# Folding the sums of four scans into the last scan's own accumulation, with the turning, the norm's bias and the sign bytes rearranged

## The chip, the cores and the metric

One core of one Trainium2 chip. The metric is the device time of one execution in microseconds (us). Every time below is a median of several executions; all of them were in the fast state. A verdict of "faster" or "slower" needs 2%.

## The reference, cut to what matters

A vision block on 4 images of 64 x 64 pixels and 96 channels: a sign-quantized projection to 192 channels, a 3 x 3 convolution, a selective scan over the 4096 pixels in four directions, a norm, a gate and another quantized projection; then an attention block and a feed-forward block, which the change does not touch.

```python
x_flat = xconv.reshape(Bn, Dn, L)
x_tr = xconv.transpose(0, 1, 3, 2).reshape(Bn, Dn, L)          # columns first
xs = concatenate([x_hwwh, flip(x_hwwh)], axis=1)               # four directions
h = dA * h + (dt * ut)[..., None] * Bt[:, :, None, :]          # the scan, 16 states
y = einsum('bkdn,bkn->bkd', h, Ct)                             # sum over the states
out_y = y + D[None, :, :, None] * u
...
y = out_y[:, 0] + inv_y[:, 0] + wh_y + invwh_y                 # the four directions
y = (y - mu) / sqrt(var + 1e-05) * ln_w + ln_b
y = y * silu(z)
return bilinear(y, W_out, s_out, b_out)                        # signs of y only
```

## The kernel before

One loop runs over 1536 pieces: 4 images, 4 directions in the order 1, 3, 0, 2, 4 chunks of 1024 pixels, 6 groups of 32 channels, 4 quarters of the states. A piece is: ScalarE (ACT) makes the decay `dA`, GpSimd (POOL) the input product, VectorE (DVE) the scan, DVE or POOL the product with C, and TensorE (PE) sums the states in PSUM (`yp`). After every eighth piece ACT copies `yp` out (`ys`) and DMAs store it to `yd`. All loads of the loop are issued on one queue, SyncE's (SP).

```python
def reduce(self, i):                       # state sums of one piece
    ...
    for x in range(4):
        c.nc.tensor.matmul(y[32 * x : 32 * x + 32, g % 2, :], c.sum4, prod[:, 256 * x : 256 * x + 256],
            start=(q == 0), stop=(q == NQ - 1), tile_position=(0, 32 * x))

def run(self, back):
    ...
    for i in range(n):
        self.at = i
        self.loads(i)                      # every 4th piece: two loads of 512 KB (dl), a few groups ahead
        if i >= 1: self.carry(i - 1)
        if i + 1 < n: self.decay(i + 1)    # ACT
        ...                                # evacuate, reduce, inject
        self.scan(i)                       # DVE
        ...
        interleave(lanes)
        next(back, None)                   # one step of the background work
```

`back` is the background: convolution and signs of the image after next (`prologue`), turning two directions back into row order (`turn`), and the eight sums of each image (`norm`, 512 pixels each), one step per piece. When the scans are over, what is left runs alone.

```python
# prologue: the signs, two bytes of a pair apart
nc.scalar.activation(sg.bitcast(F8).rearrange("p (h e i) -> p h i e", h=8, e=2),
                     pz.rearrange("p (h i e) -> p h i e", h=8, e=2), AF.Sign, saturate=False)

# turn: y1 + y3 by two products with the identity, then a strided copy out of PSUM
for i, t in enumerate(ts):
    nc.tensor.matmul(ps, c.i96, t, start=(i == 0), stop=(i == 1))
yield
nc.scalar.copy(yh.rearrange("p (h w) -> p h w", w=IW)[:, :, 8 * q : 8 * q + 8],
               ps.rearrange("p (w h) -> p h w", h=IH))

# norm, inside the scans: four products and a copy for each half
mm(ps, [(c.i96, x["y0"][:, h]), (c.i96, x["y2"][:, h]), (c.i96, x["y13"][:, h]), (c.dskip[:, h], x["u"][:, h])])
yield
nc.scalar.copy(t, ps)                      # ysum
...
mm(ps, [(c.meanw[:, 0, h], ys[0]), (c.meanw[:, 1, h], ys[1]), (c.lnb[:, h], sd)])   # sy
```

Of the kernel before, what the change touches and what calls it, by code (L numbers as in the profile page):

```python
# [37 lines left out]

KORD = (1, 3, 0, 2)
AHEAD = 4  # L40

# [9 lines left out]
def hybrid_kernel(ctx: ExitStack, tc: tile.TileContext, a: dict, out: bass.AP):  # L51
# [4 lines left out]
    def pool(name, bufs, **kw):  # L56
# [4 lines left out]
        w=pool("wp", 9), y=pool("yp", 2), cy=pool("cyp", 2), h=pool("hp", 2), pu=pool("pup", 1), pd=pool("pdp", 2),  # L61
# [80 lines left out]
    mean, meanw = ctile("mean", [96, 2, 96]), ctile("meanw", [96, 2, 2, 96])  # L142
    dskip, lnb = ctile("dskip", [96, 2, 96]), ctile("lnb", [96, 2, 96])
    on192, on96, mean96 = ctile("on192", [96, 96]), ctile("on96", [96, 96]), ctile("mean96", [96, 96])
# [6 lines left out]

    tts = [ctile(f"tt{i}", [DM + 1, 512]) for i in range(2)]

    def weights():
# [62 lines left out]
        for rows, h, s in halves(a["pv"][:, :, LN_W]):  # L217
            nc.sync.dma_start(wrow[:, h, rows], s.partition_broadcast(96))
        small = {}
# [26 lines left out]
        for tt in tts:  # L246
            nc.gpsimd.memset(tt[DM : DM + 1, :], 1.0)
# [94 lines left out]
        for h in range(2):  # L342
            for o in range(2):
                nc.vector.tensor_tensor(meanw[:, h, o], mean[:, int(h != o)], wrow[:, o], ALU.mult)
            nc.vector.tensor_scalar(dskip[:, h], i96, dsum[:, h : h + 1], None, ALU.mult)
            nc.vector.tensor_scalar(lnb[:, h], i96, pv[:, h, LN_B : LN_B + 1], None, ALU.mult)
# [11 lines left out]
    c.ready, c.later = set(), Later(nc)  # L358
# [56 lines left out]
def run(c):  # L415

    made, first = c.weights(), prologue(c, 0, c.xts)
    lanes = [made, first]
    while (0, 1) not in c.ready:
        interleave(lanes)  # L420
        c.later.tick()
    scans = Scans(c)
    ends = [Epilogue(c, b, scans) for b in range(NB)]

    def back():

        yield from first
        yield from prologue(c, 1)
        for b in range(NB):
            if b + 2 < NB:  # L430
                yield from prologue(c, b + 2)
            while not scans.done(b, 2):
                yield
            yield from turn(c, b)
            e = ends[b]
            e.open()
            yield from e.sums(e.lane)
            if b + 1 < NB:
                yield from e.middle()
                yield from e.last(e.lane)  # L440
                e.close()

    behind = back()
    scans.run(behind)


    def drain(lanes):
        while lanes:
            interleave(lanes)
            c.later.tick()  # L450
        c.later.flush()

    e = ends[-1]
    e.alone = True
    more = [e.spare_lane(x) for x in range(2)]
    drain([behind] + [e.sums(ln) for ln in more])
    drain([e.middle()])
    drain([e.last(ln) for ln in [e.lane] + more])
    e.close()


def prologue(c, b, xts=None):
# [11 lines left out]
    with tc.tile_pool(name=f"xg_{b}", bufs=1) as xgp:  # L474
# [4 lines left out]
        with tc.tile_pool(name=f"cv_{b}", bufs=1) as cvp:  # L479
# [72 lines left out]
            for n, part in enumerate(parts + [None]):  # L552
# [5 lines left out]
                for s in range(3):  # L558
# [8 lines left out]
                    if prev:  # L567
# [4 lines left out]
                        elif s == 1:  # L572
# [3 lines left out]
                                sg.bitcast(F8).rearrange("p (h e i) -> p h i e", h=8, e=2),  # L576
                                pz.rearrange("p (h i e) -> p h i e", h=8, e=2), AF.Sign, saturate=False,
# [145 lines left out]
def turn(c, b):  # L723

    nc, tc, p = c.nc, c.tc, c.p

    def load(h, q):
        ts = []
        for k in (1, 3):
            t = p.f.tile([128, 512], F32, name=f"yt{h}{q}{k}_{b}", tag="f")[0:96]  # L730
            nc.sync.dma_start(t, c.yd[k][b][96 * h : 96 * h + 96, 512 * q : 512 * q + 512])
            ts.append(t)
        return ts

    with tc.tile_pool(name=f"tn_{b}", bufs=1) as tn:
        for h in range(2):
            yh = tn.tile([96, L], F32, name=f"yh{h}_{b}", tag="yh")
            nxt = load(h, 0)
            for q in range(NQ8):
                ts, nxt = nxt, load(h, q + 1) if q + 1 < NQ8 else None  # L740
                yield
                ps = p.ps.tile([128, 512], F32, name=f"tn{h}{q}_{b}", tag=f"b{q % 2}")[0:96]
                for i, t in enumerate(ts):
                    nc.tensor.matmul(ps, c.i96, t, start=(i == 0), stop=(i == 1))  # L744
                yield
                nc.scalar.copy(
                    yh.rearrange("p (h w) -> p h w", w=IW)[:, :, 8 * q : 8 * q + 8],
                    ps.rearrange("p (w h) -> p h w", h=IH),
                )
            nc.sync.dma_start(c.y13[b][h], yh)  # L750
            yield


class Epilogue:
# [9 lines left out]
    def open(self):  # L764
        c, p, b = self.c, self.c.p, self.b
        ep = self.ep = self.ctx.enter_context(c.tc.tile_pool(name=f"ep_{b}", bufs=1))
        self.vks = ep.tile([DM, DM], F32, name=f"vks_{b}", tag="vks")
        self.ms = [ep.tile([DM + (i == 2), DM], F32, name=f"m{i}_{b}", tag=f"m{i}") for i in range(3)]
        self.lane = SimpleNamespace(
            f32=lambda nm: p.f.tile([128, 512], F32, name=f"{nm}_{b}", tag="f"),  # L770
            bank=lambda nm, j: p.ps.tile([128, 512], F32, name=f"{nm}_{b}", tag=f"b{j}"),
            load=lambda key, nm, shape, dt=F32: ep.tile(shape, dt, name=f"{nm}_{b}", tag=key),
            tts=c.tts, x={},
        )
        self.opened = True
# [4 lines left out]
    def spare_lane(self, n):  # L780
# [14 lines left out]
        for i, nm in enumerate(("y0", "y2", "y13", "u")):  # L795
            views[nm] = big[i][0:96].rearrange("p (h l) -> p h l", h=2)
# [12 lines left out]
    def take(self):  # L809
# [4 lines left out]
        if self.scans.at <= (self.b * NK + NK - 1) * NPC + NG * NQ * (ci + 1) + 16:  # L814
            return None
        return self.todo.pop(0)

    def loads(self, ln, q, names):
        c, b = self.c, self.b
        cols = slice(512 * q, 512 * q + 512)  # L820
        for nm in names:
            src, shape, dt = {
                "y0": (c.yd[0][b].rearrange("(h p) l -> p h l", h=2), [96, 2, 512], F32),
                "y2": (c.yd[2][b].rearrange("(h p) l -> p h l", h=2), [96, 2, 512], F32),
                "y13": (c.y13[b].rearrange("h p l -> p h l"), [96, 2, 512], F32),
                "u": (c.ud[b].rearrange("h p l -> p h l"), [96, 2, 512], F32),
# [4 lines left out]
            c.nc.sync.dma_start(t, src[..., cols])  # L831
# [13 lines left out]
    def sums(self, ln):  # L845
        nxt = None
        while nxt is not None or self.todo or not self.opened:
            q, nxt = nxt, None
            if q is None:
# [4 lines left out]
                self.loads(ln, q, ("y0", "y2", "y13", "u", "sz", "xb"))  # L854
# [6 lines left out]
    def norm(self, ln, q, got):  # L861
# [9 lines left out]
        ys = []  # L871
        if self.alone:
            nc.gpsimd.tensor_tensor(x["y0"], x["y0"], x["y2"], ALU.add)
            for h in range(2):
                c.vec.scalar_tensor_tensor(
                    x["y13"][:, h], x["u"][:, h], c.dsum[:, h : h + 1], x["y13"][:, h], ALU.mult, ALU.add
                )
            for h in range(2):
                t = f32(f"ysum{h}")
                c.vec.tensor_tensor(t, x["y0"][:, h], x["y13"][:, h], ALU.add)  # L880
                ys.append(t)
            yield
        else:
            for h in range(2):
                ps = bank(f"ys{h}", h)[0:96]
                mm(ps, [(c.i96, x["y0"][:, h]), (c.i96, x["y2"][:, h]), (c.i96, x["y13"][:, h]), (c.dskip[:, h], x["u"][:, h])])
                yield
                t = f32(f"ysum{h}")
                nc.scalar.copy(t, ps)
                ys.append(t)  # L890
        nxt = self.take()
        got.append(nxt)
        if nxt is not None:
            sz, xb = x["sz"], x["xb"]
            self.loads(ln, nxt, ("y0", "y2", "y13", "u"))
        sz, xb = x["sz"], x["xb"]
        sq = []
        if self.alone:
            ps = bank("mu", 0)[0:96]
            mm(ps, [(c.on192, ys[0]), (c.on192, ys[1])])  # L900
# [16 lines left out]
        ps = bank("var", int(self.alone))[0:96]  # L917
# [5 lines left out]
        sd = f32("sd")  # L923
        nc.scalar.activation(sd, ps, AF.Ln, bias=c.eps5[0:96])
# [3 lines left out]
        if self.alone:  # L928
# [4 lines left out]
            gs = yc  # L933
        else:
            for h in range(2):
                ps = bank(f"sy{h}", 1 - h)[0:96]
                mm(ps, [(c.meanw[:, 0, h], ys[0]), (c.meanw[:, 1, h], ys[1]), (c.lnb[:, h], sd)])
                sy.append(ps)
            yield
            yield  # L940
# [5 lines left out]
        yield  # L946
        gt = []
# [144 lines left out]
class Scans:  # L1092
# [6 lines left out]
    def __init__(self, c):  # L1099
# [9 lines left out]
        self.us, self.gs, self.at, self.loaded = {}, {}, -1, set()  # L1109

    def done(self, b, n):

        return self.at > (b * NK + n) * NPC + 16
# [141 lines left out]

    def reduce(self, i):
# [5 lines left out]
        y, prod = self.ydone[i // 8], self.ins.pop(i)  # L1262
        for x in range(4):
            c.nc.tensor.matmul(  # L1264
                y[32 * x : 32 * x + 32, g % 2, :], c.sum4, prod[:, 256 * x : 256 * x + 256],
                start=(q == 0), stop=(q == NQ - 1), tile_position=(0, 32 * x),
            )

# [14 lines left out]
    def run(self, back):  # L1283
# [25 lines left out]
        for i in range(n):  # L1309
            self.at = i  # L1310
            self.loads(i)
            if i >= 1:
                self.carry(i - 1)
            if i + 1 < n:
                self.decay(i + 1)
            full = i % 8 == 3 and i > 8
            if full:
                self.evacuate(i - 4)
            elif i >= 3:
# [11 lines left out]
            if full:  # L1331
                self.reduce(i - 3)
# [81 lines left out]
```

## Time and profile before

| | before |
|---|---|
| median of 3 runs | 5783.25 us (5775.27 to 5783.98) |
| profiled execution: span | 5775.5 us, mean granted clock 0.672 |
| up to the first scan of the loop | 287.9 us |
| the 1536 pieces | 5321.9 us |
| after the last scan (the tail) | 165.7 us |

The two engines that fill the loop are DVE and POOL; the prediction below shows the lines. What is worth keeping in mind when reading them: in the loop both engines are busy some 5025 us, so the time between 5025 and 5322 us is the most that a change can win there if it leaves the work of these two as it is.

A direction is 96 pieces. From the starts of the scan instructions in the time line I took the time of each of the 16 directions, and put together the first three directions of each image and its last one, which is where the change adds work:

| us, profile of before | image 0 | image 1 | image 2 | image 3 | sum |
|---|---|---|---|---|---|
| first three directions | 1021.3 | 1018.9 | 996.4 | 961.7 | 3998.3 |
| last direction | 339.5 | 335.2 | 329.8 | 319.1 | 1323.6 |

### The profile page before, as it was taken

How to read it: one execution, taken by the hardware profiler on the slowest of the kernel's cores; microseconds unless marked ns; L12 is line 12 of the kernel's file. 1: busy time of each engine (PE TensorE's matmuls, PEld its weight loads, DVE VectorE, ACT ScalarE, POOL GpSimd, SP SyncE). 2: the span in 40 equal slices, each digit the busy share in tenths (PEclk: the TensorE clock that was granted, in tenths of full speed). 3: DMA queues.
4: the chain of work that ended last, by engine and by line, in shares of the span. 5: the costliest groups of instructions: out<-in, count | busy, mean ns of one | idle time of the engine just before them, and what ended most of it. 6: DMA issues, size and time to landing. Idle time of an engine off the chain costs nothing. (4 is left out here: it accounts for less than half of the span.)

```text
span 5775.5 us, 61921 instructions
## 1 busy us (share of the span) xinstructions
PE 3419.4 (59%) x19813; PEld 1339.9 (23%) x19813; DVE 5176.7 (90%) x3422; ACT 3672.1 (64%) x5620; POOL 5080.7 (88%) x2291
## 2 busy tenths in 40 slices
PE   6446645664468755666446875563477654353577
PEld 3222222222223322222212322221122211111123
DVE  3299999999889999999999999999999999999984
ACT  5567876886556566788655656755556676554544
POOL 2099999999889999999998999999999999999980
PEclk8666755676678866666567885565688765565687
DMA  4455656655676655665567665575667555575652
GB/s 75 105 169 189 196 180 200 194 170 178 200 222 213 205 177 176 204 189 164 184 218 226 209 206 177 182 223 190 207 195 214 191 189 185 174 222 180 197 160 73
DMA packets 589452, 1069.91 MB, mean 185 GB/s; under 512 B 225867, under 2 KB 295556, under 8 KB 587332
## 3 DMA queue, kind: packets, MB, share of 16 engines
q1 hardware_dynamic: 575636, 1065.88, 59.3%
q8 instruction: 156, 2.56, 0.2%
q10 hardware_dynamic: 13488, 0.07, 0.1%
q14 instruction: 172, 1.41, 0.1%
HBM read 833.20 MB, written 229.38 MB: 184 GB/s over the span
## 5 line engine op out<-in xcount | busy, mean ns | idle before, releaser
L386 POOL TENSOR_TENSOR w<-dl,bc 128x1024 f32<-128x1024 f32 x1536 | 3578.4, 2354 | 149.2 <-PE yp L1264 73.8
L1223 ACT ACTIVATE dA<-dl,anm 128x1024 f32<-128x1024 f32 x1536 | 1714.0, 1116 | 494.6 <-DVE w L386 254.6
L1264 PE MATMUL yp<-w,sum 128*32 128x256 f32 x12288 | 1323.3, 547 | 845.8 <-ACT ys L1276 447.7
L386 DVE TENSOR_TENSOR_SCAN dA<-dA,cy,w 128x1024 f32<-128x1024 f32 x680 | 1593.1, 2343 | 109.7 <-ACT dA L1223 94.0
L386 POOL TENSOR_TENSOR w<-h,bc 128x1024 f32<-128x1024 f32 x631 | 1483.8, 2352 | 191.6 <-DVE h L386 181.0
L386 DVE TENSOR_TENSOR w<-dA,bc 128x1024 f32<-128x1024 f32 x905 | 1108.6, 1225 | 57.9 <-DVE dA L386 0.9
L386 DVE TENSOR_TENSOR_SCAN h<-dA,cy,w 128x1024 f32<-128x1024 f32 x472 | 1103.8, 2340 | 12.0 <-ACT dA L1223 10.2
L1264 PEld LDWEIGHTS yp<-w,sum 128*32 128x32 f32 x12288 | 363.1, 137 | 1941.0 <-issue 836.8
L386 DVE TENSOR_TENSOR_SCAN dA<-dA,w 128x1024 f32<-128x1024 f32 x225 | 513.6, 2283 | 38.3 <-ACT dA L1223 29.9
L1254 ACT COPY cy<-dA 128x1 f32<-128x1 f32 x680 | 105.8, 156 | 666.2 <-DVE w L386 665.7
L562 PE MATMUL cv<-tp,cw 96*96 96x512 fp8e5 x1152 | 390.8, 499 | 137.5 <-ACT r L611 110.0
L386 DVE TENSOR_TENSOR_SCAN h<-dA,w 128x1024 f32<-128x1024 f32 x159 | 362.3, 2279 | 32.0 <-POOL w L386 23.7
L562 PEld LDWEIGHTS <-cw 96*96 96x96 fp8e5 x1152 | 174.3, 158 | 358.2 <-issue 314.6
L744 PE MATMUL tn<-yt,ident 96*96 96x512 f32 x256 | 175.1, 820 | 111.8 <-DMA yt<-yd 111.1
L836 PE MATMUL ys<-ey,ident 96*96 96x512 f32 x336 | 184.7, 692 | 75.2 <-DMA ey<-yd 47.4
L1254 ACT COPY cy<-h 128x1 f32<-128x1 f32 x472 | 87.6, 186 | 193.5 <-DVE h L386 193.5
L575 ACT ACTIVATE sg<-cz 96x512 fp8e5<-96x512 f32 x64 | 159.0, 2484 | 22.1 <-DVE cz L386 22.0
L1166 ACT ACTIVATE pd<-dps,dbias,pvd 128x512 f32<-128x512 f32 x189 | 143.7, 760 | 23.1 <-PE dps L1161 23.1
L386 DVE TENSOR_TENSOR u<-cz,e 96x512 f32<-96x512 f32 x64 | 43.8, 684 | 115.6 <-ACT e L586 108.6
L1167 ACT ACTIVATE sp<-dps,dbias,pvd 128x512 f32<-128x512 f32 x189 | 144.6, 765 | 0.0
L836 PE MATMUL fc<-x,mean 96*96 96x512 f32 x54 | 51.9, 1064 | 151.9 <-DVE x L386 151.9
L386 DVE TENSOR_TENSOR pd<-dps,pu 128x512 f32<-128x512 f32 x189 | 130.7, 691 | 8.6 <-DMA pu<-ud 2.2
(305 smaller groups left out, 4448.1 us busy)
## 6 DMA issues: line engine op xcount, KB each, us to landing
dl<-dld SPq DMA_DIRECT2D x768, 512.0 KB
bc<-bcd SPq DMA_DIRECT2D x512, 512.0 KB
dld<-pd SPq DMA_DIRECT2D x126, 512.0 KB
yd<-ys SPq DMA_DIRECT2D x768, 64.0 KB
dld<-pd SPq DMA_DIRECT2D x126, 256.0 KB
yt<-yd SPq DMA_DIRECT2D x128, 192.0 KB
ey<-yd SPq DMA_DIRECT2D x58, 384.0 KB
pu<-ud SPq DMA_DIRECT2D x32, 512.0 KB
```

Source lines behind the costliest of these rows:

```text
L386: return getattr(self.eng, name)(out, *args, **kw)
L562: nc.tensor.matmul(ps, c.cw[:, j, t, 96 * h : 96 * h + 96], tpad[j][:, 8 * q + dy : 8 * q + dy + 8, dx : dx + IW], start=(j == 0 and t == ...
L575: nc.scalar.activation(sg.bitcast(F8).rearrange("p (h e i) -> p h i e", h=8, e=2), pz.rearrange("p (h i e) -> p h i e", h=8, e=2), AF.Sign ...
L744: nc.tensor.matmul(ps, c.i96, t, start=(i == 0), stop=(i == 1))
L836: self.c.nc.tensor.matmul(ps, w, x, start=(i == 0), stop=(i == len(pairs) - 1))
L1166: nc.scalar.activation(d[:, 0], ps, AF.Abs, scale=sc, bias=bi)
L1167: nc.scalar.activation(t, ps, AF.Relu, scale=sc, bias=bi)
L1223: c.nc.scalar.activation(t, self.dlt[i // NQ][0], AF.Exp, scale=c.anm[:, g, NQ * KORD[e] + q : NQ * KORD[e] + q + 1])
L1254: self.c.nc.scalar.copy(self.carries[g, q], h[:, CH - 1 : CH])
L1264: c.nc.tensor.matmul(y[32 * x : 32 * x + 32, g % 2, :], c.sum4, prod[:, 256 * x : 256 * x + 256], start=(q == 0), stop=(q == NQ - 1), tile ...
```

## The change

Its intent is to take work off ACT and PE inside the loop. The last direction's state sums are already being accumulated in PSUM; the y of the other directions and D u are added there by a few more products, so that the sum of all four directions is stored as `yd[2]` and the norm needs one load and no sum of its own. Five parts:

1. Sign bytes in order: `sg` is written contiguously, PSUM is read with a step of two.
2. `load_sums`: in direction 3 the y of direction 1 is added (one product per group), in direction 2 y0, the turned y and u D (three products). `ysum` goes.
3. Turning without products: `yh` is copied straight from the loaded tile, which holds y1 + y3 already.
4. The norm's bias is row 97 of the product `sy` and not a product of its own.
5. Order and tail: sums may start 8 pieces after their chunk instead of 16, and in the last 64 pieces the background takes two steps per piece. Two more turns of order belong here: `turn` now comes ahead of `prologue` of the image after next, not behind it, and the copy `ys` stands ahead of the next decay in ACT's order, not behind it. No run takes either of these two alone.

```diff
-    sg.bitcast(F8).rearrange("p (h e i) -> p h i e", h=8, e=2),
-    pz.rearrange("p (h i e) -> p h i e", h=8, e=2), AF.Sign, saturate=False,
+    sg.bitcast(F8).rearrange("p (h e i) -> p h e i", h=8, e=2),
+    pz.rearrange("p (h i e) -> p h e i", h=8, e=2), AF.Sign, saturate=False,
 ...
+    def load_sums(self, i):
+        b, e, ci, g, q = self.pieces[i]
+        k = KORD[e]
+        if k < 2:
+            return
+        at = CH * (NCH - 1 - ci)
+        t = c.p.ya.tile([128, 3, 256], F32, name=f"ya_{i}", tag="ya")          # pool of one buffer
+        srcs = [c.yd[1][b]] if k == 3 else [c.yd[0][b], whole(c.y13[b]), whole(c.ud[b])]
+        for j, src in enumerate(srcs):
+            c.nc.sync.dma_start(t[:, j], src[32 * g : 32 * g + 32, at : at + CH].rearrange("d (x l) -> x d l", x=4))
+        self.sums[i // NQ] = [(t[:, j, ::-1], c.dskip[:, g] if j == 2 else c.back4) for j in range(len(srcs))]
 ...  # reduce
+        for n, (src, w) in enumerate(more):
+            c.nc.tensor.matmul(y[:, g % 2, :], w, src, start=False, stop=(n == len(more) - 1))
 ...  # run
             self.loads(i)
+            if i % NQ == NQ - 1:
+                ...
+                self.load_sums(i)
 ...
+            if i % 8 == 3 and i > 8:
+                self.evacuate(i - 4)           # the copy ys, now ahead of self.decay(i + 1)
 ...
             next(back, None)
-            if full:
-                self.reduce(i - 3)
+            if i > n - 64:
+                next(back, None)
 ...  # turn
-                for i, t in enumerate(ts):
-                    nc.tensor.matmul(ps, c.i96, t, start=(i == 0), stop=(i == 1))
-                yield
-                nc.scalar.copy(yh..., ps.rearrange("p (w h) -> p h w", h=IH))
+            nc.scalar.copy(yh..., ts.pop(0).rearrange("p (w h) -> p h w", h=IH))
+            if n + 3 < len(parts):
+                ts.append(load(*parts[n + 3]))
 ...  # norm
-                mm(ps, [(c.i96, x["y0"][:, h]), (c.i96, x["y2"][:, h]), (c.i96, x["y13"][:, h]), (c.dskip[:, h], x["u"][:, h])])
-                nc.scalar.copy(t, ps)
-                mm(ps, [(c.meanw[:, 0, h], ys[0]), (c.meanw[:, 1, h], ys[1]), (c.lnb[:, h], sd)])
+                mm(ps, [(c.meanw[0:96, 1, h], ys[1]), (c.meanw[:, 0, h], y0)])
```

## The prediction

> **What bounds the kernel now.** I read the page's busy line first, then the windows of three stretches (start, scans, tail), then the 16 windows of one scan direction each, then who waited for whom, then the time line around single stalls and of the tail.
>
> ```profile
> PE 3419.4 (59%) x19813; PEld 1339.9 (23%) x19813; DVE 5176.7 (90%) x3422; ACT 3672.1 (64%) x5620; POOL 5080.7 (88%) x2291
> ```
>
> ```profile
> 0.00:285.00 285.00, 152.84 (x711) 87.71 (x712) 74.94 (x135) 148.86 (x197) 41.14 (x104) 0.75 0.40 87
> 285.00:5613.00 5328.00, 3160.13 (x18778) 1204.93 (x18777) 5027.10 (x3152) 3457.35 (x5312) 5029.11 (x2181) 0.67 0.61 193
> 5613.00:5776.00 163.00, 106.46 (x332) 47.31 (x324) 74.70 (x135) 65.87 (x112) 10.49 (x7) 0.72 0.33 89
> ```
>
> The columns are length, then busy time and instructions of PE, PEld, DVE, ACT, POOL. The 1536 scan pieces take 5328 us (3.47 us each). DVE is busy 5027 of them and POOL 5029: both are full and balanced, and each lies idle 5.6%. The start (285 us) and the tail (163 us) stand alone. So the time is 5030 us of DVE and POOL work that this change hardly touches, about 300 us of their gaps, and 448 us of ends. Of the 16 directions the worst is the last of image 0, with the turning and the first state sums behind it, and the best has nearly nothing behind it:
>
> ```profile
> 1286.00:1618.00 332.00, 155.59 (x1204) 65.58 (x1206) 299.30 (x181) 208.77 (x324) 299.75 (x131) 0.61 0.62 190
> 4613.00:4945.00 332.00, 161.76 (x1054) 57.64 (x1054) 323.08 (x199) 215.57 (x339) 322.95 (x140) 0.61 0.55 182
> ```
>
> DVE idles 33 us in the first and 9 in the second. If all 16 were like the best, 16 x 9 = 144 of the 300 us would stay, so background work can cost about 150 us at most. The waits inside the scans say through whom:
>
> ```profile
> DVE dA L386 <- ACT dA L1223: 123.9, 82, 8.5
> DVE u L386 <- ACT e L586: 44.3, 28, 3.4
> ...
> ACT ysum L889 <- PE ys L836: 138.9, 52, 11.0
> ACT yh L746 <- PE tn L744: 44.6, 18, 10.6
> ```
>
> ACT is 64% busy yet late: it takes its work in order, so a copy that waits for PE holds back the next decay (dA), and DVE has two dA buffers only. One such stall in full, at the first sum of image 0:
>
> ```profile
> 1675.12 5.40 PE L836 MATMUL ys<-ey,ident 96*96 96x512 f32 x6 [10.46 <-DMA ey<-yd]
> ...
> 1681.55 0.58 ACT L889 COPY ysum<-ys 96x512 f32<-96x512 f32 x1 [9.60 <-DMA dld<-pd]
> ...
> 1683.31 2.30 DVE L386 TENSOR_TENSOR_SCAN dA<-dA,w 128x1024 f32<-128x1024 f32 x1 [7.04 <-ACT dA L1223]
> ```
>
> PE waits for the six loads, ACT for PE, DVE for ACT. I went through all DVE waits on ACT in the scans (209 us) in the time line and sorted them by the ACT idle just ahead: a copy of ysum 67 us (48 waits), u behind the sign bytes 44 us (28), a copy of yh 18 us, plain ones with no such cause 44 us, others the rest.
>
> **What the Trainium skill says.** "Perfetto Trace Analysis", section Identifying the Most-Contended Engine: for Vector and GPSIMD occupancy is a fair measure of the distance to the roof; here both stand at 94% within the scans, which agrees with a small possible gain. "SBUF — State Buffer", section Door 1: The DMA port swizzle: SBUF is accessed in 16-byte lines and an access that moves to a new line each time is penalised. The trace agrees:
>
> ```profile
> L575 ACT ACTIVATE sg<-cz 96x512 fp8e5<-96x512 f32 x64 | 159.0, 2484 | 22.1 <-DVE cz L386 22.0
> L598 ACT COPY ut<-u 96x512 f32<-96x512 f32 x48 | 52.9, 1101 | 41.9 <-DVE u L386 41.9
> L746 ACT COPY yh<-tn 96x512 f32<-96x512 f32 x64 | 36.9, 577 | 54.4 <-PE tn L744 44.6 <-DMA bc<-bcd 6.8 <-issue 3.0
> ```
>
> sg writes single bytes 32 bytes apart (2484 ns, against 770 for other fp8 results); ut reads SBUF 256 bytes apart (1101); yh reads PSUM in the same stride without a penalty (577). "FP8 and Floating Point Precision", section TensorE Precision Notes: true fp32 takes 4 passes. The trace agrees: an fp32 product of 512 columns shows as two records, 0.43 us each at the faster clock.
>
> **The change part by part.**
> 1. Sign bytes in order: 64 x sg. The bytes are now written in order and PSUM is read with a step of two. Busy time should fall from 2484 to 770-950 ns; in the time line its slot falls from 1.95 us (131.56 to 133.52) to about 0.65, so 1.3 us each. In the scans the 28 waits of u shrink by up to 1.3 us: 44 to about 11, **-33**. In the start the loop of the 16 convolution parts is 7.45 us, of which the ACT and DVE chain (0.77 r, 0.94, 1.95 sg, 0.95, 0.66, 0.66, u 0.69, v 0.81) makes all; shortened it is 6.15. But PE's own loop is the convolution plus about 1.9, and the convolution takes 4.08 us in some parts, 5.8 to 7.4 in the others. Only the fast parts gain: **-6**.
> 2. State sums into the scans' PSUM: the 4 fp32 products and the copy of ysum, per half and 512 columns, go (56 copies x 581 ns of ACT, 246 us of PE records), with their 67 us of DVE stalls. What takes their place is the wait of the square for yc and the first load: I keep 17 us, **-50**. Added: 96 groups in direction 3 with one product and 96 in direction 2 with three, 384 fp32 products of 128 x 256, an estimate of 0.43 to 0.85 us each by the passes, 165 to 330 us of PE, against 478 that go with turning (175), ys (246) and the bias (57). Loads: 384 x 128 KB = 50 MB come, 12.6 (turning) and 29 x 3 x 384 KB = 34 MB go; a wash. The new load is asked for three pieces (10.4 us) ahead and has one buffer; PE will wait for it at times, and POOL and ACT have about three pieces of slack: **+10**.
> 3. Turning without products: 64 yh copies read SBUF in a 256-byte stride, so like ut 1.10 instead of 0.58 us: +34 us of ACT, and ACT itself waits for the load. The lead from load to copy is three pieces as before, so its 18 us of DVE stalls stay: **0**.
> 4. Bias as a row: 57 us of PE off the path, the sy product has 97 rows: **0**.
> 5. Order and tail. Before, four of image 3's eight sums are left at the last scan (yc of four is seen before 5590), so the tail has a round of three and a round of one:
>
> ```profile
> 5613.43 0.58 ACT L1276 COPY ys<-yp 128x512 f32<-128x512 f32 x1 [4.35 <-PE yp L1264]
> ...
> 5675.31 0.25 DVE L386 TENSOR_TENSOR vks<-vk,vks 96x96 f32<-96x96 f32 x1
> ...
> 5698.78 0.25 DVE L386 TENSOR_TENSOR vks<-ln0ps,vks 96x96 f32<-96x96 f32 x1 [5.64 <-PE ln0ps L836]
> ```
>
> A sum has 13 yields before and 11 after, the settling time is 8 pieces instead of 16, and the last 64 pieces take two steps each. By counting, sums 7 to 2 finish inside the scans and two are left: one round. Loads from 5616 land by about 5620, and a lone round takes 27 us (5672 to 5699) less 3 for the adds, plus 6 for two lanes: done near 5650 instead of 5699: **-45**. The last stage (76 us) is unchanged. The price is norm work at twice the pace: about 17 us of PE in 5.5 pieces beside the scans' products, and ACT waiting within one piece: **+15** for six sums.
>
> The scans' DVE gains, 33 + 50 = 83, count for 70, because POOL lies idle for other reasons too (74 us for PE). Sum: -70 + 10 + 15 - 45 - 6 = -96. 5783 - 96 = 5687; I say **5690 us**.
>
> **Rivals.** (a) The stalls move instead of going: ACT now waits for loads in turning, the square waits for yc and ys. For it: every stall above 7 us began at a load. Then -40 in place of -70, and with the tail 5720. (b) The double pace at the end costs what the tail gains: each step that waits within its own piece can cost DVE 1 to 2 us, five such steps in six sums are 40. Then about 5715. (c) The added sums are late in PE: the product frees late, POOL starves and ACT's copy of the state sums, now ahead of the decay, stalls. For it: 23 waits of PE for the turning loads, up to 13.7 us. Against it: three pieces of slack. 192 groups at 0.5 us would be +96: no gain. (d) Relief of PE and ACT reaches nearly all of the 150 us that the background costs: -120 in the scans, 5640.
>
> **Range and chances.** Most of the sum is certain in sign; sizes are not. With (d) and a cheap tail 5620; with (a) and (b) together 5745. 2% is 116 us, below 5668, 22 us past my middle: faster 0.31, same 0.67, slower 0.02.
>
> **What would show it.** sg near 0.8-0.95 us; yh near 1.1; no ysum and no tn; scans' DVE idle near 220 us and u's wait on e near 11; new waits of PE yp on ya few and below 10 us; two sums after the last scan and the tail near 118 us instead of 163; the start near 279. It is wrong if DVE's wait for dA stays at 124 (rival a), if the idle in the last 64 pieces passes 30 us (b), or if POOL waits for PE above 74 (c).

## The result, and the profile after

The changed kernel takes 5724.14 us (median of 4 runs, 5703.31 to 5737.8) against 5782.82 us (4 runs) before. The ratio is 0.9898, with a 95% interval of 0.9865 to 0.9931: about 1% faster, within the 2%. A ratio is the mean time of one kernel's fast runs over that of the other's fast runs of the same rounds, so it is not quite the ratio of the medians. The changed kernel's runs scatter over 34 us, before's over 9; the profiled execution (5737.8 us) is the slowest of the four, so stretches read from it are up to some 15 us long in all. The start varies little, 259 to 269 us in all profiles with the signs in order, and the tail with the double pace 118 to 124, so most of these 15 us are probably in the loop.

First the busy line of the page of the changed kernel, then the windows of its start, its loop, its tail and the last 64 pieces (columns as in the prediction: length, busy time and instructions of PE, PEld, DVE, ACT and POOL, granted clock, DMA share, GB/s):

```profile
PE 3345.6 (58%) x19813; PEld 1357.2 (24%) x19813; DVE 5154.9 (90%) x3396; ACT 3566.8 (62%) x5564; POOL 5075.9 (88%) x2295
```

```profile
0.00:267.10 267.10, 144.55 (x739) 85.76 (x740) 78.04 (x139) 121.38 (x198) 42.32 (x104) 0.78 0.44 96
267.10:5613.80 5346.70, 3112.89 (x18796) 1231.45 (x18795) 5025.60 (x3161) 3393.00 (x5278) 5029.30 (x2188) 0.65 0.61 194
5613.80:5736.00 122.20, 88.19 (x278) 39.98 (x278) 51.23 (x96) 52.44 (x88) 4.32 (x6) 0.73 0.22 63
5356.60:5613.80 257.20, 190.16 (x884) 80.78 (x884) 210.30 (x138) 130.96 (x204) 206.66 (x90) 0.77 0.51 161
```

The first scan of the loop comes at 267.2 us:

```profile
267.18 4.59 DVE L401 TENSOR_TENSOR_SCAN h<-dA,w 128x1024 f32<-128x1024 f32 x2 [16.61 <-POOL w L401]
```

So the start is 21 us shorter (267.2 against 287.9) and the tail 43 us (122.2 against 165.7). The loop, where ACT lost 63 us of work and where my terms came to a gain of 45 us (-70 + 10 + 15), is 25 us longer in this execution. The same two engines do as much work there as before, so their gaps grew: DVE lies idle for 321 us of it instead of 295. By directions:

| us, profile of after | image 0 | image 1 | image 2 | image 3 | sum | against before |
|---|---|---|---|---|---|---|
| first three directions | 995.7 | 980.1 | 974.1 | 973.5 | 3923.4 | -74.9 |
| last direction | 361.8 | 359.1 | 339.2 | 363.0 | 1423.1 | +99.5 |

The twelve directions without the new triple products gained 75 us, near the 83 that I had put down for the sign bytes and the sums together. The four last directions gave 100 us back. The windows of the last direction of image 0, before and then after:

```profile
1309.20:1648.70 339.50, 163.31 (x1237) 66.65 (x1240) 307.35 (x185) 207.12 (x322) 307.30 (x135) 0.61 0.63 193
```

```profile
1262.90:1624.70 361.80, 226.22 (x1439) 101.84 (x1436) 316.85 (x200) 226.35 (x354) 316.40 (x140) 0.67 0.65 201
```

Ten of the 22 us are DVE work that fell into another direction before, since the order of the background changed (15 more DVE instructions); 13 are idle time of DVE (45 us instead of 32). Who waits for whom in the loop of the changed kernel (us in total, times, longest), first DVE's list, then ACT's:

```profile
DVE dA L401 <- ACT dA L1219: 127.8, 77, 9.3
DVE h L401 <- ACT dA L1219: 49.2, 16, 9.0
...
DVE u L401 <- ACT e L601: 2.3, 7, 0.4
```

```profile
ACT sq L904 <- PE yc L847: 95.4, 54, 10.0
ACT ys L1292 <- PE yp L1283: 71.6, 36, 5.8
```

DVE's wait for the sign bytes fell from 44.3 to 2.3 us, and ysum is gone from ACT's list. Yet DVE's waits for the decay (both lines) went from 141.8 us (123.9 for `dA`, and 17.9 for `h`) to 177.0. ACT's list holds the reason: the copy of the state sums, `ys`, which waited for PE 4.3 us in the loop before, now waits 71.6 us there, behind the added products (L1283). These in turn wait for their loads. The view of the tile `ya` says so (who waited for it, us, times), and so does the group of the added products with weight `back`:

```profile
  PE yp L1283: 275.0, 165
  ACT ys L1292: 81.7, 37
```

```profile
L1283 PE MATMUL yp<-ya,back 128*128 128x256 f32 x576 | 289.4, 616 | 252.9 <-DMA ya<-yd 237.1 <-DMA ya<-y 15.5
```

One such stall in full, from the time line of the last direction of image 0 (start, duration, engine, line, instruction; in brackets the idle time before it and what ended it):

```profile
1323.37 1.24 SPq L1196 DMA_DIRECT2D dl<-dld  x2
1324.70 0.56 SPq L1264 DMA_DIRECT2D ya<-yd  x1
...
1331.40 1.22 PE L1283 MATMUL yp<-ya,back 128*128 128x256 f32 x2 [4.03 <-DMA ya<-yd]
...
1334.73 1.22 PE L1283 MATMUL yp<-ya,dskip 128*128 128x256 f32 x2 [0.41 <-DMA ya<-ud]
1335.99 0.58 ACT L1292 COPY ys<-yp 128x512 f32<-128x512 f32 x1 [4.07 <-PE yp L1283]
1336.47 1.12 ACT L1219 ACTIVATE dA<-dl,anm 128x1024 f32<-128x1024 f32 x1
1337.70 2.30 DVE L401 TENSOR_TENSOR_SCAN dA<-dA,w 128x1024 f32<-128x1024 f32 x1 [2.29 <-ACT dA L1219]
```

SP issues two loads of 512 KB and then, 1.3 us later, the first load of the sums (128 KB). It is 6.7 us from that issue until PE can start on it, and PE had been ready for 4.03 us, so of the 10.4 us that the code seems to leave only 2.7 were left at the issue. SP's own waits tell where they went: in its order the dl loads come first, and these must wait until ACT has read the buffer they overwrite (that wait is not new, 891.8 us in before; what is new is a load behind it that PE needs three pieces later).

```profile
SPq L1196 <- ACT dA L1219: 827.2, 186, 13.1
```

PE, then ACT in its fixed order, then DVE stand still one after the other, the same chain as with ysum before, only with another head.

### The profile page after: what moved, and what is told of

Same layout as the page of the kernel before. It is cut to its first block, busy times and chain, and to the rows that moved or that the text cites. A ratio compares the mean times of both kernels' runs of the same rounds, so it can differ in the third digit from the quotient of the medians.

```text
span 5736.0 us, 62039 instructions
## 1 busy us (share of the span) xinstructions
PE 3345.6 (58%) x19813; PEld 1357.2 (24%) x19813; DVE 5154.9 (90%) x3396; ACT 3566.8 (62%) x5564; POOL 5075.9 (88%) x2295
## 2 busy tenths in 40 slices
DMA packets 613245, 1069.92 MB, mean 187 GB/s; under 512 B 225083, under 2 KB 343924, under 8 KB 611124
## 5 line engine op out<-in xcount | busy, mean ns | idle before, releaser
L1278 PE MATMUL yp<-w,sum 128*32 128x256 f32 x12288 | 1355.0, 550 | 983.2 <-POOL w L401 531.6
L1278 PEld LDWEIGHTS yp<-w,sum 128*32 128x32 f32 x12288 | 345.0, 135 | 2046.6 <-POOL w L401 817.2
L1283 PE MATMUL yp<-ya,back 128*128 128x256 f32 x576 | 289.4, 616 | 252.9 <-DMA ya<-yd 237.1
L577 PE MATMUL cv<-tp,cw 96*96 96x512 fp8e5 x1152 | 376.1, 481 | 88.6 <-ACT r L626 83.9
L1283 PEld LDWEIGHTS yp<-ya,back 128*128 128x128 f32 x576 | 133.0, 278 | 425.7 <-DMA ya<-yd 304.6
L1292 ACT COPY ys<-yp 128x512 f32<-128x512 f32 x192 | 112.4, 586 | 94.5 <-PE yp L1283 81.7
L847 PE MATMUL yc<-eys,mean 96*96 96x512 f32 x240 | 137.5, 726 | 34.9 <-DMA eys<-yd 27.5
```

The costliest lines, as they stand in the source:

```text
L577: nc.tensor.matmul(ps, c.cw[:, j, t, 96 * h : 96 * h + 96], tpad[j][:, 8 * q + dy : 8 * q + dy + 8, dx : dx + IW], start=(j == 0 and t == ...
L847: self.c.nc.tensor.matmul(ps, w, x, start=(i == 0), stop=(i == len(pairs) - 1))
L1283: c.nc.tensor.matmul(y[:, g % 2, :], w, src, start=False, stop=(n == len(more) - 1))
L1292: c.nc.scalar.copy(t, y[:, :, ::-1] if k >= 2 else y)
```

## The experiments

Gains are given as (1 - ratio) x 5776 us, 5776.01 us being the median of before in the first set of runs. That compares each kernel with before on the same chip in the same rounds; the four sets ran on four chips, whose before lies between 5771.82 and 5778.03 us. An interval is about +-8 us for most, but +-19 us for the changed kernel itself.

| run | what it is | median us | ratio (95%) | gain us |
|---|---|---|---|---|
| | the changed kernel | 5724.14 | 0.9898 (0.9865 to 0.9931) | 59 |
| e1_sg_alone | before, with the sign bytes in order | 5723.56 | 0.9907 (0.9891 to 0.9922) | 54 |
| e2_sums_no_load | changed, sums from a fixed tile (wrong on purpose) | 5651.29 | 0.9779 (0.9764 to 0.9794) | 128 |
| e3_sums_first | changed, loads of the sums ahead of the dl loads | 5696.01 | 0.9853 (0.9836 to 0.9871) | 85 |
| e4_single_pace | changed, one step per piece to the end | 5700.12 | 0.9865 (0.9851 to 0.988) | 78 |
| e5_sums_early | changed, loads of the sums a group earlier, two buffers | 5697.97 | 0.987 (0.9857 to 0.9884) | 75 |
| e6_early_single | e5 and e4 | 5674.04 | 0.9827 (0.9813 to 0.984) | 100 |
| e7_old_sg | changed, with the sign bytes apart again | 5764.03 | 0.9978 (0.9968 to 0.9989) | 13 |
| e8_early_single_wait | e6, the first sum's loads two steps earlier than its use | 5660.14 | 0.9805 (0.9792 to 0.9819) | 113 |
| e9_turn_products | changed, turning with a product per part again | 5703.85 | 0.9871 (0.9852 to 0.9889) | 75 |
| e10_du_earlier | e8, D u added a direction earlier | 5635.53 | 0.9751 (0.9733 to 0.9769) | 144 |
| e11_best_no_load | e8, sums from a fixed tile (wrong on purpose) | 5614.3 | 0.972 (0.9702 to 0.9739) | 162 |
| e12_best | e10 and e9's turning | 5609.18 | 0.9723 (0.971 to 0.9736) | 160 |

All but the two that say so gave the right result. My theory after the result: the sign bytes gain what they gain, the sums' relief is real, and the late loads of the added sums and the double pace give most of it back. The rivals: the sums' relief was never there (it was only the sign bytes); the added products are too much for PE, whatever their loads do; the added DMA traffic is the price, not its lateness.

Not all of my expectations, quoted below, came true: e1, e2, e10, e11 and e12 gained more than I had said, e5 gave its rival's number, e7 lies just below my range and in its rival's, and e8 lies between the two. e3, e4, e9 (the third of its cases) and the difference of e6 to e5 came as one of the cases had it.

### The sign bytes alone, and everything but them

The first takes before and changes two lines, the second takes the changed kernel and changes them back.

```diff
-    sg.bitcast(F8).rearrange("p (h e i) -> p h i e", h=8, e=2),
-    pz.rearrange("p (h i e) -> p h i e", h=8, e=2), AF.Sign, saturate=False,
+    sg.bitcast(F8).rearrange("p (h e i) -> p h e i", h=8, e=2),
+    pz.rearrange("p (h i e) -> p h e i", h=8, e=2), AF.Sign, saturate=False,
```

> The kernel before with the sign bytes written in order and nothing else. My theory: u no longer waits behind sg in the scans (44 us of waits before, 2 in the changed kernel), so the scans lose 25 to 33 us and the start 8 to 9: 5740 to 5750 us. Rival: DVE only waits elsewhere once u's wait is gone, only the start's gain stays: 5774 us.

> The changed kernel with only the old byte order of sg put back: the sum of all other parts. If the parts add, it lies 52 us above the changed kernel and equals the kernel before: 5768 to 5784 us, that is, the other four parts together bring nothing. Rival: ACT now has room (no ysum copies), so the old sg costs less there than it did before: 5745 to 5765 us.

Alone they gain 54 us, and the changed kernel without them keeps 13 us of its 59. So two lines are nearly the whole result, and the other four parts together are worth 5 to 13 us (6 to 18 by the interval of e7). The group of `sg` in the changed kernel, against the 159.0 us and 2484 ns of before (busy us, mean ns | idle before):

```profile
L590 ACT ACTIVATE sg<-cz 96x512 fp8e5<-96x512 f32 x64 | 37.5, 586 | 24.0 <-DVE cz L401 23.9
```

586 ns (588 in e1) is below the 770 to 950 I had expected, so each saves 1.9 us in this list, where I had taken 1.3 from the time line. In e1's profile the loop is 35 us shorter than in before's (5286.5 against 5321.9), close to the 33 of the prediction, and DVE's wait for `e` is 24.5 us of it (19.8 us instead of 44.3; expected: 11). The start is where the prediction was short: 26 us less (first scan at 261.4), where it had 6. Counted from one `sg` to the next, the 15 steps of the first image's convolution take 118.3 us in before, 94.0 in e1 and 97.3 in the changed kernel. A short step falls from 7.4 to 5.8 us, and the five long ones of 8.5 to 9.2 us are gone too: none is above 7.5 in e1. (PE's longer convolutions, 5.8 to 7.4 us a part in before, take 5.8 there after the first of 5.9; why they became shorter is not shown.)

### The loads taken away, or only earlier

e2 keeps the products and their order and takes the loads alone away, by reading a fixed tile of zeros:

```diff
-        t = c.p.ya.tile([128, 3, 256], F32, name=f"ya_{i}", tag="ya")
+        if not hasattr(self, "fixed"):
+            self.fixed = c.p.ya.tile([128, 3, 256], F32, name="ya_fixed", tag="ya")
+            c.nc.gpsimd.memset(self.fixed, 0.0)
+        t = self.fixed
 ...
-            c.nc.sync.dma_start(t[:, j], src[...])
+            pass
```

> The changed kernel with the same added products, but from one fixed tile set to zero and without the loads of the others' y and of u (result wrong on purpose). If late loads of these tiles are what made direction 2 slower by 27 us in images 0 and 1, by 10 in image 2 and delayed the tail, this comes to 5680 to 5695 us. If the added PE work or the moved prologue is the cause, it stays within 10 us of the changed kernel (5724).

It is 69 us faster than the changed kernel. DVE's waits for the decay in the loop:

```profile
DVE dA L401 <- ACT dA L1219: 80.2, 67, 4.2
DVE h L401 <- ACT dA L1219: 26.0, 11, 5.8
```

106.2 us instead of 177.0, a difference of 71 us, about the gain. So the products themselves fit in PE. The rival that the relief was never there falls too: the 128 us of e2 are 31 more than the sign bytes (54) and the tail (43) bring together, and the double pace and the turning, which cost time (below), are still in it. What remained was which side of the loads hurts: that they are late, or that they are there. Two kernels ask for them sooner, one by turning the order of two statements, one a whole group (four pieces) ahead with two buffers. The buffer's room comes from the pool of `ys`.

```diff
 # e3, in run
             self.at = i
-            self.loads(i)
             if i % NQ == NQ - 1:
                 ...
                 self.load_sums(i)
+            self.loads(i)
 # e5, in run, against the changed kernel; ya gets two buffers, ys one
             self.at = i
-            self.loads(i)
-            if i % NQ == NQ - 1:
+            j = i + NQ
+            if i % NQ == NQ - 1 and j < n:
                 ...
-                self.load_sums(i)
+                self.load_sums(j)
+            self.loads(i)
```

> The changed kernel with the load of the sums' tile asked for ahead of the same piece's 1 MB of delta loads instead of behind them. If the lateness is that queue (the delta load waits for ACT's last decay and then moves 1 MB), PE's waits for the tile fall from about 300 us to below 100 and the time to 5695 to 5710 us. If it is the transfer's own latency or the single buffer, nothing changes: 5715 to 5730 us.

> The changed kernel with two buffers for the sums' tile (the scans' output tile gives up its second one for the room) and its loads asked for a whole group earlier, ahead of the delta loads: seven pieces of lead instead of three, and the queue no longer blocked by the single buffer. If waiting (PE for the tile, the queue for the buffer) is what the loads cost, this comes close to the run without loads (5651 us): 5655 to 5670. If it is their 50 MB and 48000 packets in the queues that delay all other loads, it stays near the run with the order alone turned (5696): 5685 to 5700.

The tile view of `ya`, first in e3, then in e5:

```profile
  PE yp L1283: 65.0, 59
  ACT ys L1292: 33.0, 18
```

```profile
  ACT ys L1292: 27.8, 15
  PEld yp L1283: 8.4, 12
```

The order of two statements brings 26 us and takes PE's wait from 275 to 65 us. "DMA: Bandwidth & Descriptors", section Queues, rings and completion order, in the Trainium skill states that SP owns one row of rings, one on each DMA engine, and that on each engine descriptors are consumed in ring order; a load behind 1 MB of others then comes behind them. The two runs agree with that: the same loads, asked for before the dl loads instead of after them, make PE wait a quarter as long. They do not show it alone, though, since in e3 these loads no longer stand behind SP's wait ahead of the dl loads either. That wait falls from 827 to 473 us, while SP's wait for the sums' one buffer rises from 86 to 295 us. But e5, where PE hardly waits for them at all, gains no more than e3 (75 and 85 us, within each other's intervals). So of the 69 us that the loads cost, lateness is some 16 to 26, and 43 to 53 remain with the loads there and in time. (The single buffer of `ys` in e5 does not account for them: in its list ACT's copy waits for no store of `ys`.) In the last direction of image 0 the DMA share of the window is 0.60 in e2 and 0.68 in e5 (windows below, e2 first), and its time 341.2 and 356.0 us:

```profile
1250.60:1591.80 341.20, 207.83 (x1446) 101.91 (x1445) 316.67 (x200) 226.21 (x354) 315.49 (x140) 0.71 0.60 186
```

```profile
1251.00:1607.00 356.00, 203.97 (x1443) 100.61 (x1436) 316.72 (x201) 226.38 (x354) 315.63 (x140) 0.72 0.68 205
```

The busy times of DVE are equal; the difference is idle time of DVE, 25 against 39 us. The whole program moves as much as before the change (1069.92 MB against 1069.91), but the loads that went had lain for the larger part in other directions, while the new loads, 96 of 128 KB in direction 3 and 288 in the last direction, crowd three quarters of themselves into one quarter of the time.

### The pace at the end

e4 takes the second step per piece away; the branch for running alone is then chosen once per sum, since it could otherwise switch within one.

```diff
+        alone = self.alone                     # norm: used in place of self.alone below
 ...
             next(back, None)
-            if i > n - 64:
-                next(back, None)
```

> The changed kernel with one step a piece also in the last 64 pieces. Theory: the double pace costs 40 us in the last 64 pieces (260.7 us against 220.5 before) and saves no second round, only one lane of three in the last one: the last 64 pieces come to 222 to 230 us, the tail from 122 to 130 us, the time to 5690 to 5700 us. Rival: the tail gets back a second round (27 us) and the added products keep the last pieces slow: 5715 to 5735 us.

> The same, and one step a piece in the last 64 pieces. The two effects are in different stretches, so they should add: 24 us below e5, 5632 to 5648 us if e5 is at 5655 to 5670. Rival: with early loads the double pace hurts less (PE waits less in the last pieces), so only 5 to 12 us below e5.

Without the double pace the changed kernel gains 19 us by the ratios, and in one and the same set e6 gains 25 us over e5. The windows of the last 64 pieces, first of before and then of e4, beside the 257.20 us of the changed kernel above (the 260.7 and 220.5 us of the expectation are of windows that begin one piece earlier):

```profile
5392.70:5609.80 217.10, 152.60 (x760) 57.15 (x760) 205.74 (x129) 122.10 (x188) 201.72 (x88) 0.79 0.56 171
```

```profile
5342.90:5565.10 222.20, 167.39 (x828) 70.94 (x829) 207.56 (x134) 125.12 (x193) 204.18 (x90) 0.79 0.59 184
```

The double pace costs 35 us in the last 64 pieces (257.2 against 222.2). What DVE waited for there in the changed kernel (none of these three is in before's list for its last 64 pieces; the line left out is the decay, 7.9 us against before's 7.7):

```profile
DVE g L401 <- PE sy L847: 14.9, 7, 4.7
DVE vks L401 <- PE vk L847: 8.6, 5, 2.3
...
DVE tt L401 <- ACT xr L853: 6.0, 2, 3.0
```

With two steps per piece a DVE instruction of the norm follows the PE or ACT instruction that feeds it within the same piece, and DVE, which takes its work in order, stands still for it. In return the tail is only 13 us shorter than with the single pace (122.2 against 134.8 us): the larger part of the tail's gain, 31 us of 43, comes without it.

### Hiding a first load, and spreading the added loads

In ACT's list the largest wait for PE was that of the square for `yc`, 95.4 us in 54 waits. Part of it arises because the first sum of each round reads its load two steps after asking for it; e8 adds two steps. (There the square waits 63.4 us in 42 waits, the longest 4.1 us instead of 10.0.) e10 then moves one of the three loads and products of the last direction into the direction before it, where none are added (that direction runs forward, so its part of the load and its weight are no longer reversed; these lines are left out):

```diff
 e8
                 self.loads(ln, q, ("ys", "sz", "xb"))
                 yield
                 yield
+                if not self.alone:
+                    yield
+                    yield
 e10
-        if k < 2:
+        if k == 1:
             return
-        srcs = [c.yd[1][b]] if k == 3 else [c.yd[0][b], whole(c.y13[b]), whole(c.ud[b])]
+        srcs = {3: [c.yd[1][b]], 0: [whole(c.ud[b])], 2: [c.yd[0][b], whole(c.y13[b])]}[k]
```

> e6 with two more pieces between the first loads of an image's state sums and their first use. In the changed kernel ACT's square waited once an image up to 10 us for products that wait for this load (9.6 to 14.5 us). If DVE's stall there is real on the chain, this takes 5 to 8 us for each of the first three images: 15 to 24 us below e6. Rival: the stall moves to the next load, nothing within 5 us.

> e8 with D u added in the direction before the last instead of in the last: the same loads and products in all, but at most two loads for each group of the last direction instead of three. If what is left of their cost is crowding in the last direction of images 0 and 1 (351 and 345 us there in e8, against 342 and 339 without loads), the time falls to 5645 to 5654 us. If the cost goes with the bytes wherever they lie, it stays at 5655 to 5666.

> e8 without the loads of the sums' tile (products from a fixed zero tile, result wrong on purpose): what the loads still cost where PE does not wait for them. If their cost is traffic that delays the other loads, and the longer wait at the first state sum hides part of it, 5620 to 5635 us (25 to 40 below e8). If the only cost was the waiting that early loads and the longer wait removed, 5648 to 5660.

e8 gains 13 us over e6, e10 another 31 over e8, with not a byte or a product less. So spreading them is worth something by itself: in the profiles the last directions fall from 1349.2 to 1316.1 us in sum (351.8 to 339.6 in image 0, 347.1 to 340.2, 333.2 to 322.8, 317.2 to 313.6), while the first three of each image rise from 3912.7 to 3920.1. e11, without any loads of sums but with all three products in the last direction, is 18 us better than e10 and 49 better than e8: so it was the loads there and not the products that cost, and 31 of the 49 us went when one load in three was moved. (The fixed tile holds zeros; that this does not help by a faster clock shows in the mean granted clock, 0.666 in e8 and 0.665 in e11.) Whether what the crowded loads cost comes through the DMA traffic or through SP's one queue is not shown. I have looked at one wait only: in the last direction of image 0 PE's `yc` waited for its load 9.6 us in e2 and 14.5 in the changed kernel.

### The turning, and all of it together

e9 puts one product with the identity back between the load and the copy, so that `yh` reads PSUM; the copy comes one step later than in the changed kernel, so the run changes the lead by a piece as well.

```diff
-            nc.scalar.copy(yh..., ts.pop(0).rearrange("p (w h) -> p h w", h=IH))
+            if prev:
+                finish(*prev)                  # nc.scalar.copy(yh..., ps.rearrange("p (w h) -> p h w", h=IH))
+            ps = p.ps.tile([128, 512], F32, name=f"tn{h}{q}_{b}", tag=f"b{q % 2}")[0:96]
+            nc.tensor.matmul(ps, c.i96, ts.pop(0), start=True, stop=True)
+            prev = (yh, h, q, ps)
```

> The changed kernel with the turning's product put back (one per part, lead of the loads unchanged): ACT's copy reads PSUM again, 577 instead of 1080 ns, 64 of them, and PE has 64 fp32 products more. If turning without products is worth something by itself (no PE in the way of ACT), this is slower by 8 to 20 us: 5732 to 5744. My prediction gave it 0: 5716 to 5732 us. If the slower copy costs more than the product did, it is faster: 5700 to 5715.

> The version with early sums, single pace, two waits and D u a direction earlier (5635.5 us) plus turning with one product per part again, as in the kernel before. If the effects add, because they lie in different stretches (turning in the start of each direction and the stages between images, the sums in the last directions), the 15 to 20 us that turning with products gained over the changed kernel come on top: 5615 to 5622 us. Rival: with fewer stalls left, the turning's evictions no longer hold VectorE up and it gains nothing: 5630 to 5640 us.

The groups of `yh` in the changed kernel and in e9:

```profile
L754 ACT COPY yh<-yt 96x512 f32<-96x512 f32 x64 | 69.1, 1080 | 23.1 <-DMA yt<-yd 23.1
```

```profile
L752 ACT COPY yh<-tn 96x512 f32<-96x512 f32 x64 | 36.9, 577 | 25.4 <-PE tn L766 25.3
```

ACT is relieved of 32 us; what the product costs PE does not show as a loss. The waits before the copies are nearly the same (23.1 and 25.4 us), so the lead matters little by this line. In the third direction of each image, where alone the turning runs in these kernels, DVE's idle time falls from 55.6 us in the changed kernel to 42.7 in e9, and from 65.2 in e10 to 48.1 in e12. The rest of e9's gain in its profile lies in directions that do not turn and is not explained. e9 gains 16 us over the changed kernel, which the wide interval of the latter alone would leave in doubt; e12 over e10 gains 16 us again by the ratios (26 by the medians, with before 3 us faster in that set). e12 is 2.8% faster than before and 1.8% faster than the changed kernel (0.9723 against 0.9898). In it DVE's wait for the decay is down to half:

```profile
DVE dA L401 <- ACT dA L1233: 63.8, 46, 3.3
```

## Why the prediction was right or wrong

The prediction was right in its verdict and its range (5724 us within 5620 to 5745, the middle 34 us too low), but by a sum whose terms were not right one by one, and so with some luck. In the two profiled executions the start came out 15 us better than said (-21 us instead of -6), the tail 2 us worse (-43 instead of -45), and the loop 70 us worse (+25 instead of -45); by the medians the loss in the loop is some 20 us smaller.

| step of the prediction | said | the runs showed |
|---|---|---|
| sign bytes, scans and start | -33 and -6 | -54 in all (e1; in its profile -35 in the loop and -26 in the start); -46 within the changed kernel (e7) |
| relief of the state sums | -50 | not run alone; some -80 by an estimate (below) |
| added products and their loads | +10 | +69 for the loads (e2) |
| turning without products | 0 | +16 (e9), +16 again in e12 |
| bias as a row | 0 | not run alone |
| tail | -45 | -43 |
| double pace | +15 | +35 in the loop for 13 us of tail; net +19 (e4), +25 (e6) |

**Right, and for the reason given.** The tail: two sums were left, the last of them was done at 5655 us, 41 us after the last scan, and the tail is 122 us, near the 118 I had put down. The engine lists: no ysum, no tn, `yh` at 1080 ns (said: 1.1 us). The sign bytes in the scans, -35 in e1's profile against -33.

**Sizes that were off.** The sign bytes were under-sized in the start. The step was "Only the fast parts gain: -6": I held PE's own loop with its convolution of 5.8 to 7.4 us against the long parts. But the start is 26 us shorter in e1 and 21 in the changed kernel, against 1 us in e7, which has the old sign bytes (first scan at 286.9); the long steps became shorter as well as the short ones (118.3 to 97.3 us for 15 steps). The added products fill 380 us of PE's records (289.4 with `back`, 90.4 with `dskip`), above the estimate of 165 to 330, and yet e2 shows room for them. (The 0.43 us of the prediction is the pace of fp32 records one behind the other; a record by itself lasts 0.59 us or more in before.) The turning's step failed at "+34 us of ACT ... 0": the 32 us of ACT were right, but I let them count for nothing on an engine of which I had just said that it is late although it is 64% busy. Part (b) of the rivals, a double pace that costs what it gains, came true, by its own sign (DVE's idle time in the last 64 pieces is 47 us, over the 30 named): 35 us in the loop, where I had put +15 in the sum. In the reading of the profile one thing was wrong: the worst stretch, the last direction of image 0, has the turning behind it but not "the first state sums"; by the time line 14 of that image's 16 squares fall into the direction after it.

**The step that failed.** "The new load is asked for three pieces (10.4 us) ahead and has one buffer; PE will wait for it at times, and POOL and ACT have about three pieces of slack: +10", and before it "Loads: ... a wash". Two things were wrong in it. The load is asked for after two 512 KB loads of the same piece, which I did not look at: the queue must first be free to issue those, and then the load comes behind them. In the stall shown 2.7 us of the 10.4 were left at the issue, and the load took 6.7. And a balance of megabytes over the whole program says nothing of a stretch: 288 of the 384 loads fall into the four last directions. ACT had no slack of three pieces either, since `ys` stands in its order ahead of the next decay. My sign of failure, "new waits of PE yp on ya few and below 10 us", shows it best: none was over 9.2 us (9.7 for its weight loads), but there were 165, 275 us in all. So does the sign for the loop, "scans' DVE idle near 220 us": it is 321.

**Of the rivals.** (a) is half right: the waits for the decay did not go down (127.8 us for `dA`, as before), but by moving to the added sums, not to turning; its other half came true, the square's wait for `yc` rose from 41.2 to 95.4 us. (c) came true for ACT's copy, which it had named, and not for POOL, whose wait for PE fell from 74 to 17 us. The waits that it brought up for itself were waits for loads, which was the right sign; but its size, +96, is near the +69 by chance, since it was reckoned from the products, and e2 shows that these fit. (d), the full relief at 5640 us, is near what the same change brings once its loads and pace are put right: e10 and e12 lie at 5636 and 5609.

What the relief of the sums is worth can only be estimated: -54 for the signs, +69, +16, +22 for the pace and -31 for the tail without it make +22, so the measured -59 leaves -81 for it. The profiles come near that. The first three directions of all images are 42 us shorter in the changed kernel than in e1 (3923.4 against 3964.9), and this with the turning's 16 us in them and some 20 us of the added loads (they are 20 us shorter in e2, 3903.4): 78 in all. The changed kernel's scatter of 34 us is large beside such differences of single executions.

## What to carry to other kernels

When work moves to where its data must be loaded again, look at what the queue issues just ahead of that load and at the traffic of that stretch, not at the program's total of bytes; asking before the big loads, and spreading the additions over the stretches, was worth more here (26 and 31 us) than the four other parts as they were first put together. Time on an engine that takes its work in order is not free because the engine is 64% busy, when each item of it stands ahead of something that the full engine waits for. And when several edits come in one change, run the smallest alone: two lines here brought 54 us, and the other four parts together about 5 to 13, with gains and losses of some 110 us each inside them by the estimate above.

## What the Trainium skill lacked or had wrong

- "SBUF — State Buffer", section Door 1: The DMA port swizzle, says that leaving a 16-byte line is penalised, but gives no size for ScalarE, and none for writes. Here 512 bytes per partition written by turns 32 bytes apart took 2484 ns, in order 586 ns: 3.7 ns more per byte element. Reading 512 fp32 from SBUF 256 bytes apart took 1080 ns against 577 to 586 ns without that stride: 1.0 ns more per element.
- The same section says of PSUM that access out of line slows matmuls; no page that I read tells what it does to ScalarE. Here it does nothing: ScalarE read PSUM with a step of two in 586 ns (`sg`) and 256 bytes apart in 577 ns (`yh` in before and e9), as fast as contiguously (586 ns, `ys`).
- "DMA: Bandwidth & Descriptors", section Queues, rings and completion order, tells the order of consumption but not what a small load pays behind large ones: here a 128 KB load issued 1.3 us after two of 512 KB was used 6.7 us after its issue, and the other order took PE's waits for these loads from 275 to 65 us.
